# The router's pick with its scores, keys and sums in PSUM

## The chip, the cores and the metric

The kernel runs on one core of one Trainium2 chip. The metric is device time in microseconds (us) for one execution of the whole program, the median over several runs. One further execution was taken with the hardware profiler; every duration of a single instruction below is from that execution.

The engines are named as in the profile: PE is TensorE (PEld its weight loads), DVE is VectorE, ACT is ScalarE, POOL is GpSimd, SP is SyncE, which only issues DMA transfers here.

## The reference

One layer of two parts, on 8 batches of 256 rows of 512 numbers (2,048 rows, called tokens below). All is float32.

```python
x = x + xattn(layernorm(x), k, fside, ctx, ctx, 8)
x = x + ffn(layernorm(x), gate_w, ...)

# xattn: a causal convolution of products, then a sum over one index
kv = vr[:, :, :, None, :] * x2r[:, :, None, :, :]
y = irfft(rfft(kv) * k_f)[..., :L] + kv * skip
out = einsum('bhijl,bhil->bhjl', y, x1r)

# ffn: a shared expert, and the best two of eight experts for each token
scores = sigmoid(xf @ gate_w.T)
topk_w, topk_idx = top_k(scores, 2)
topk_w = topk_w / (topk_w.sum(-1, keepdims=True) + 1e-20) * 2.5
shared_out = silu(xf @ shared_wg.T) * (xf @ shared_wu.T) @ shared_wd.T
h = silu(einsum('td,efd->etf', xf, exp_wg)) * einsum('td,efd->etf', xf, exp_wu)
picked = einsum('etf,edf->etd', h, exp_wd)[topk_idx, arange(T)[:, None]]
routed_out = (topk_w[..., None] * picked).sum(axis=1)
```

## The kernel before

**Two stages.** In the first, up to about 462 us, a loop runs over the 32 heads of the convolution (`for h in range(H)`, L735). For each head, TensorE multiplies a Toeplitz tile by the products `kv` in ten matmuls that fill four PSUM tiles, `cv_0` to `cv_3` (`conv_products`, L306); GpSimd makes `kv` two heads ahead with four multiplications (`make_kv`, L292), and every other head the skip products with two more (L342, L344); VectorE weighs each PSUM tile with one multiplication and one reduction (`weigh`, L321: L326, L332). `ps_cv` has three buffers (L92), so a `cv` tile can be written once L326 has read the one three tiles before it. Between the heads TensorE does the matmuls of the shared expert (`up_step`, `down_step`). In the second stage the routed tokens are worked off in 39 blocks of 128 rows, each with the weights of its expert.

**The order is written out by hand** (`tc.manual_schedule()`, L79): each engine runs its instructions in the order of the program. What an instruction waits for is put in by the framework from the tiles that it reads and writes.

**The router** works on four chunks of 512 tokens (`NCHUNK`, L24). A chunk takes these steps, for chunks 0 to 2 inside the heads 10 to 14, 18 to 22 and 26 to 30, for chunk 3 after the last head:

- `route_logits` (L387) and `route_T` (L400): four small matmuls, a copy, and four transposes leave the logits' partial sums in a PSUM tile `plT`, tokens along the partitions.
- `route_pick` (L410), on VectorE but for one Sigmoid on ScalarE. On tiles of 128 partitions by 4 groups by 8 experts it finds the largest score (L429), marks where it stands (L430), multiplies by a falling `rank` so that the first of equals wins (L431, L432, L433), takes it out (L435) and does the same again; then the sum of both scores and its inverse (L437 to L440), the table's entries (L444, L445), the mask of picked experts (L448) and sums of the mask over the groups (L452).
- `route_ranks` (L457): two matmuls count in PSUM how many tokens before a token go to the same expert.
- `route_places` (L477): VectorE makes each token's place in the table, and GpSimd scatters the entries with eight indirect DMAs.

After chunk 3 the table is loaded again (`load_table`, L652), and `slots` (L668) makes from it the rows that the blocks of the second stage gather.

**Where the pick stands in a head.** For head 12, 20 and 28, `route_pick` comes between the second and the third weighing:

```python
        weigh(h, 1, pss[1])
        ...
            if r == 2:
                route_pick(c)
        ...
        weigh(h, 2, pss[2])
        ...
        weigh(h, 3, pss[3])
```

`ps_tp` (L94) is a ring of two PSUM buffers, used in turn by the transposes of the residual (`ptr`, L375), `pl`, `plT`, the ranks (`rk`, L460), every other product of the shared expert's second half, and `slots_ps`. The pick's own tiles (`score`, `left`, `key`, `best`, `top`, `sel`, `den`, `entry`, `mask`, `before`) are all in SBUF, in a pool of two buffers.

Of the kernel before, what the change touches and what calls it, by code (L numbers as in the profile page):

```python
# [11 lines left out]
ALU = mybir.AluOpType  # L12
AX = mybir.AxisListType
PE = mybir.EngineType.PE

P = 128
# [6 lines left out]
NLB = L // P  # L23
NCHUNK = 4  # L24
TPC = NT // NCHUNK
TC = TPC * P
NEXP = 8
# [17 lines left out]
SCALE = 2.5  # L45
# [3 lines left out]
def tile_xattn_moe(  # L49
# [28 lines left out]
    V, G, A, T, S = nc.vector, nc.gpsimd, nc.scalar, nc.tensor, nc.sync  # L78
# [97 lines left out]
    place = const.tile([P, NEXP], F32, name="place")  # L176
# [207 lines left out]
    lg, plT, picks = {}, {}, {}  # L384
# [20 lines left out]
    shape = [P, TPC, NEXP]  # L405

    def along(t):
        return t.unsqueeze(2).to_broadcast(shape)

    def route_pick(c):  # L410
        def rt(name, s=shape, dtype=F32):
            return small.tile(s, dtype, tag=name, name=f"{name}_{c}")

        logit = rt("logit")
        V.tensor_reduce(
            logit,
            plT.pop(c).rearrange("p i (k e) -> p i e k", k=NLB)[:, :, :NEXP, :],
            AX.X,
            ALU.add,
        )  # L420
        score = rt("score")
        A.activation(score, logit, AF.Sigmoid)
        left, key, best = rt("left"), rt("key"), rt("best", [P, TPC])
        top, sel = [], []
        for n in range(2):
            src = left if n else score
            top.append(rt(f"top{n}", [P, TPC]))
            sel.append(rt(f"sel{n}"))
            V.tensor_reduce(top[n], src, AX.X, ALU.max)  # L429
            V.tensor_tensor(key, src, along(top[n]), ALU.is_equal)  # L430
            V.tensor_tensor(key, key, rank.unsqueeze(1).to_broadcast(shape), ALU.mult)  # L431
            V.tensor_reduce(best, key, AX.X, ALU.max)  # L432
            V.tensor_tensor(sel[n], key, along(best), ALU.is_equal)  # L433
            if n == 0:
                V.scalar_tensor_tensor(left, sel[0], -2.0, score, ALU.mult, ALU.add)  # L435
        den = rt("den", [P, TPC])
        V.tensor_tensor(den, top[0], top[1], ALU.add)  # L437
        V.tensor_scalar_add(den, den, 1e-20)
        V.reciprocal(den, den)
        V.tensor_scalar_mul(den, den, SCALE)  # L440

        entry = rt("entry", [P, TPC, 2, 2])
        for n in range(2):
            V.tensor_copy(entry[:, :, n, 0], tokoff[:, c * TPC : (c + 1) * TPC])  # L444
            V.tensor_tensor(entry[:, :, n, 1], top[n], den, ALU.mult)  # L445
        mask = rt("mask", [P, TPC + 1, NEXP])
        V.memset(mask[:, TPC], 0.0)
        V.tensor_tensor(mask[:, :TPC], sel[0], sel[1], ALU.add)  # L448
        before = rt("before", [P, TPC + 1, NEXP])
        V.memset(before[:, 0], 0.0)  # L450
        for i in range(TPC):
            V.tensor_tensor(before[:, i + 1], before[:, i], mask[:, i], ALU.add)  # L452
        picks[c] = (sel, entry, mask, before)
# [23 lines left out]
    def route_places(c):  # L477
        def rt(name, s=shape, dtype=F32):
            return small.tile(s, dtype, tag=name, name=f"{name}_{c}")

        sel, entry, _, _ = picks.pop(c)
        ps = ranks.pop(c)
        pos = rt("pos")
        V.tensor_tensor(
            pos, ps[:, :TPC], place.unsqueeze(1).to_broadcast(shape), ALU.add
        )
        V.tensor_tensor(place, place, ps[:, TPC], ALU.add)
        for n in range(2):
            at, to = rt("at"), rt(f"to{n}", [P, TPC], I32)
            V.tensor_tensor(at, pos, sel[n], ALU.mult)  # L490
            with nc.allow_low_precision(reason="whole numbers below 2**14"):
                V.tensor_reduce(to, at, AX.X, ALU.add)
            for i in range(TPC):
                ins = G.indirect_dma_start(  # L494
                    out=table,
                    out_offset=bass.IndirectOffsetOnAxis(ap=to[:, i : i + 1], axis=0),
                    in_=entry[:, i, n, :],
                    in_offset=None,
                    bounds_check=P * NCOL - 1,
                    oob_is_err=True,  # L500
                )
                tc.declare_no_dep(ins.ins, group="table", reason="no two rows have one place")
                tc.add_to_no_dep_group("table", ins.ins)
                scatters.append(ins)
# [230 lines left out]
    for h in range(H):  # L735
# [39 lines left out]
        c, r = divmod(h - 10, 8)  # L775
        if c >= 0:
            if r == 2:
                route_pick(c)
            if r == 4:
                route_places(c)  # L780
# [49 lines left out]
    step()  # L830
    route_T(last_c)
    route_pick(last_c)
    settle()
    step()
    route_ranks(last_c)
    route_places(last_c)
    ek, pick, used = block_experts()
    tab = load_table()
# [246 lines left out]
```

## Time and profile before

| what | value |
|---|---|
| median of 3 runs | 825.37 us (824.21 to 828.68) |
| the profiled execution | 827.25 us in all, of it 825.5 us from the first to the last instruction (the span) |
| mean granted clock of TensorE | 0.99 |
| TensorE matmuls L312 (the convolution) | 640 records, 283.5 us |
| VectorE L326 and L332 | 128 each, 87.3 and 87.8 us |
| GpSimd L298 (`kv`) | 128, 132.4 us, 1067 ns each |

The first part of the profile's page gives each engine's busy time, its share of the span and its instructions. In the list of waits a row reads: engine, tile and line that waited, after the arrow whom it waited for, then the total in us, how often, and the longest. In a timeline a row reads: start in us from the span's start, duration in us, engine, line, operation, the tile written, an arrow, the tiles read, the shapes, how many instructions are merged into the row, and in brackets the engine's idle time just before and what ended it. A VectorE duration runs from the start of the instruction to its end and includes time in which it is held up after it has started.

### The profile page before, as it was taken

What the parts mean: (1) busy time and instruction counts of PE and PEld (TensorE: products, weight loads), DVE (VectorE), ACT (ScalarE), POOL (GpSimd) and SP (SyncE); (2) the same over time, 40 slices, a digit from 0 to 9 for tenths busy, and PEclk for the clock granted to TensorE, in tenths of its full rate; (3) what the DMA queues carried; (4) which work ended last, traced back from release to release, by engine and by line L of the source; (5) the groups of instructions that cost most, each with busy time, mean ns of one, the idle gap of its engine ahead of it and who ended that gap; (6) DMA issues with size and microseconds to landing.
All of it is one profiled execution on the core that took longest, in us unless ns stands there. A gap on an engine that the chain in (4) does not pass through costs nothing. (4 is left out here: it accounts for less than half of the span.)

```text
span 825.5 us, 7804 instructions
## 1 busy us (share of the span) xinstructions
PE 796.1 (96%) x2143; PEld 388.2 (47%) x2143; DVE 565.2 (68%) x1356; ACT 117.1 (14%) x180; POOL 429.3 (52%) x425
## 2 busy tenths in 40 slices
PE   8989999999999999999999999999999999999991
PEld 4434444444444444444444444455555555555550
DVE  4869966958745958755784625349888888888860
ACT  2000111111102120012120020001111111111110
POOL 7956652319532506815412103575777777777621
PEclk9999999999999999999999999999999999999996
DMA  6473333022432030330210187159333444333332
GB/s 217 160 260 114 118 112 103 25 89 49 135 110 90 26 103 13 134 109 25 65 38 1 51 332 267 36 180 252 72 71 73 77 74 74 74 71 69 65 41 35
DMA packets 52139, 82.77 MB, mean 100 GB/s; under 512 B 8832, under 2 KB 24064, under 8 KB 50944
## 3 DMA queue, kind: packets, MB, share of 16 engines
q1 hardware_dynamic: 36960, 55.48, 20.6%
q0 software_dynamic: 10816, 18.92, 12.3%
q10 hardware_dynamic: 4320, 7.87, 2.6%
q8 instruction: 19, 0.31, 0.1%
q14 instruction: 24, 0.20, 0.1%
HBM read 60.05 MB, written 22.18 MB: 100 GB/s over the span
## 5 line engine op out<-in xcount | busy, mean ns | idle before, releaser
L312 PE MATMUL cv<-kv,tz 128*128 128x512 f32 x640 | 283.5, 598 | 10.0 <-DVE prod L326 8.1
L312 PEld LDWEIGHTS cv<-kv,tz 128*128 128x128 f32 x640 | 119.6, 191 | 158.9 <-issue 125.2
L298 POOL TENSOR_TENSOR kv<-vT,ctxT 128x512 f32<-128x512 f32 x128 | 132.4, 1067 | 92.8 <-PE cv L312 76.9
L855 POOL DMA_INDIRECT xg<-xn_d,src x144 | 146.8, 1019 | 56.6 <-issue 38.5
L914 PE MATMUL up<-wgu_sb,xT 128*128 (+1 forms) x576 | 176.1, 459 | 0.0
L522 PE MATMUL gu<-xfT,wsh 128*128 128x512 f32 x352 | 154.4, 593 | 0.0
L958 DVE STREAM_TRANSPOSE hTb<-h 32x96 f32<-32x96 f32 (+1 forms) x560 | 146.3, 261 | 8.2
L914 PEld LDWEIGHTS up<-wgu_sb,xT 128*128 128x128 f32 x576 | 109.1, 190 | 70.6 <-issue 16.4
L494 POOL DMA_INDIRECT table<-entry,to x32 | 31.8, 995 | 143.0 <-DVE at L490 134.5
L522 PEld LDWEIGHTS gu<-xfT,wsh 128*128 128x128 f32 x352 | 66.6, 190 | 83.1 <-issue 82.6
L326 DVE TENSOR_TENSOR prod<-cv,ctxT 128x512 f32<-128x512 f32 x128 | 87.3, 682 | 23.7 <-PE cv L312 22.4
L972 PE MATMUL y<-wd_sb,hTb 128*128 (+3 forms) x216 | 98.6, 593 | 0.8 <-ACT hTb L947 0.8
L332 DVE TENSOR_REDUCE convT<-prod 128x64 f32<-128x512 f32 x128 | 87.8, 686 | 4.4
L981 POOL DMA_INDIRECT out_dram<-ys,row x36 | 58.2, 1616 | 42.8 <-issue 20.1
L567 PE MATMUL dn<-wshd,hT 128*128 128x512 f32 x160 | 70.6, 593 | 0.0
L972 PEld LDWEIGHTS y<-wd_sb,hTb 128*128 128x128 f32 (+1 forms) x216 | 41.0, 190 | 43.1 <-issue 34.9
L567 PEld LDWEIGHTS dn<-wshd,hT 128*128 128x128 f32 x160 | 30.2, 190 | 37.6 <-issue 37.6
L923 DVE TENSOR_TENSOR h<-h,up 128x352 f32<-128x352 f32 x36 | 18.6, 517 | 41.3 <-ACT h L922 41.3
L539 DVE TENSOR_TENSOR sg<-sg,gu 128x512 f32<-128x512 f32 (+1 forms) x24 | 16.4, 684 | 41.8 <-ACT sg L536 41.8
L361 POOL TENSOR_TENSOR skip<-ctxT,w 128x512 f32<-128x512 f32 x16 | 17.7, 1108 | 47.7 <-DVE w L356 47.7
L922 ACT ACTIVATE h<-up 128x352 f32<-128x352 f32 x36 | 16.7, 463 | 164.4 <-PE up L914 164.4
L536 ACT ACTIVATE sg<-gu 128x512 f32<-128x512 f32 (+1 forms) x24 | 14.3, 596 | 178.6 <-PE gu L522 178.5
(131 smaller groups left out, 421.9 us busy)
## 6 DMA issues: line engine op xcount, KB each, us to landing
wgu_sb<-in_egu_dram SPq DMA_DIRECT2D x8, 1408.0 KB, 16.7
x<-in_x_dram SPq DMA_DIRECT2D x32, 256.0 KB, 3.8
tz<-in_toep_dram SPq DMA_DIRECT2D x32, 256.0 KB, 2.7
ctxT<-in_cT_dram SPq DMA_DIRECT2D x16, 256.0 KB, 4.0
xn_d<-xn ACTq DMA_DIRECT2D x16, 256.0 KB, 2.0
out_dram<-x SPq DMA_DIRECT2D x16, 256.0 KB, 2.2
wd_sb<-in_ed_dram SPq DMA_DIRECT2D x8, 512.0 KB, 12.0
xq_f<-xn_d SPq DMA_DIRECT2D x60, 64.0 KB, 2.0
```

The source lines that it names most:

```text
L298: G.tensor_tensor(kv[:, mb], vT[t][:, mb, :, cols].unsqueeze(2).to_broadcast([P, B, NH, NH]), ctxT[t][:, mb, :, cols].unsqueeze(3).to_broa ...
L312: T.matmul(ps.rearrange("p b j i -> p (b j i)"), lhsT=tz[:, (lb - mb) * P : (lb - mb + 1) * P], rhs=kv[:, mb].rearrange("p b j i -> p (b j ...
L326: V.tensor_tensor(prod, ps, ctxT[t][:, lb, :, cols].unsqueeze(2).to_broadcast([P, B, NH, NH]), ALU.mult,)
L332: V.tensor_reduce(convT[t][:, lb, :, cols], prod, AX.X, ALU.add)
L494: ins = G.indirect_dma_start(out=table, out_offset=bass.IndirectOffsetOnAxis(ap=to[:, i : i + 1], axis=0), in_=entry[:, i, n, :], in_offse ...
L522: T.matmul(ps, lhsT=wsh[:, k, m0 : m0 + m], rhs=rhs[k], start=(k == 0), stop=(k == NLB - 1))
L567: T.matmul(ps, lhsT=hTs[c][:, ft, i * P : (i + 1) * P], rhs=wshd[:, ft, :], start=(ft == 0), stop=False,)
L855: G.indirect_dma_start(out=xgs[k][:, c, :], out_offset=None, in_=xn_q, in_offset=bass.IndirectOffsetOnAxis(ap=src[:, c, k : k + 1], axis=0 ...
L914: T.matmul(ps[:, m, :FF], lhsT=xTs[k][:, j].rearrange("p c b -> p (c b)"), rhs=wk[:, bass.ds(eks[k] * NGU + (m * NLB + j) * FF, FF)], star ...
L958: V.transpose(hT[q * Q : (q + 1) * Q, :n, c], hk[c * Q : (c + 1) * Q, q * NF * Q : (q * NF + n) * Q].rearrange("p (t a) -> p t a", a=Q),)
L972: T.matmul(ps, lhsT=hT[:fw, ft].rearrange("p c b -> p (c b)"), rhs=wk[:fw, bass.ds(eks[k] * NWD + ft * L, L)], start=(ft == 0), stop=(ft = ...
L981: G.indirect_dma_start(out=out, out_offset=bass.IndirectOffsetOnAxis(ap=row[:, k : k + 1], axis=0), in_=y, in_offset=None, bounds_check=NT ...
```

## The change

It is confined to `route_pick` and `route_places`. The score, what is left of it, and the keys are views of the chunk's own PSUM tile `plT`, at columns 0, 32 and 64 of each group's 128; the second top's sum and the denominator lie at columns 96 and 97. The second top is taken twice: once into SBUF, for the entries, once into PSUM, for the sum. The addition of 1e-20 and the scaling are one instruction with the constant 1/SCALE ahead of the inverse. The comparison that gives `sel[1]` is done a second time in place on `key`, so that the mask has an operand in PSUM. In `route_places`, `pos` is written over the ranks in PSUM. VectorE issues 28 instructions in a pick where it issued 27. The order of the instructions of all other engines stays; the Sigmoid's output is now in PSUM.

```diff
+        ps = plT.pop(c)
+
+        def pt(n, m=NEXP):
+            return ps[:, :, 32 * n : 32 * n + m]
+
         logit = rt("logit")
         V.tensor_reduce(
             logit,
-            plT.pop(c).rearrange("p i (k e) -> p i e k", k=NLB)[:, :, :NEXP, :],
+            ps.rearrange("p i (k e) -> p i e k", k=NLB)[:, :, :NEXP, :],
             AX.X,
             ALU.add,
         )
-        score = rt("score")
+        score, left, key = pt(0), pt(1), pt(2)
         A.activation(score, logit, AF.Sigmoid)
-        left, key, best = rt("left"), rt("key"), rt("best", [P, TPC])
+        best = rt("best", [P, TPC])
...
-        den = rt("den", [P, TPC])
-        V.tensor_tensor(den, top[0], top[1], ALU.add)
-        V.tensor_scalar_add(den, den, 1e-20)
+        second, den = pt(3, 1)[:, :, 0], ps[:, :, 3 * 32 + 1]
+        V.tensor_reduce(second, left, AX.X, ALU.max)
+        V.tensor_tensor(den, top[0], second, ALU.add)
+        V.tensor_scalar(den, den, 1e-20, 1.0 / SCALE, ALU.add, ALU.mult)
         V.reciprocal(den, den)
-        V.tensor_scalar_mul(den, den, SCALE)
...
-        V.tensor_tensor(mask[:, :TPC], sel[0], sel[1], ALU.add)
+        V.tensor_tensor(key, key, along(best), ALU.is_equal)
+        V.tensor_tensor(mask[:, :TPC], sel[0], key, ALU.add)
...
-        pos = rt("pos")
-        V.tensor_tensor(
-            pos, ps[:, :TPC], place.unsqueeze(1).to_broadcast(shape), ALU.add
-        )
+        pos = ps[:, :TPC]
+        V.tensor_tensor(pos, pos, place.unsqueeze(1).to_broadcast(shape), ALU.add)
```

## The prediction

> **What bounds it now.** I read the page's first part, then TensorE's list of waits, then the timelines of TensorE, VectorE and GpSimd around one pick.
>
> ```profile
> PE 796.1 (96%) x2143; PEld 388.2 (47%) x2143; DVE 565.2 (68%) x1356; ACT 117.1 (14%) x180; POOL 429.3 (52%) x425
> PE cv L312 <- DVE prod L326: 8.1, 4, 3.7
> 154.39 7.99 PE L312 MATMUL cv<-kv,tz 128*128 128x512 f32 x18 [1.40 <-DVE prod L326]
> 286.50 7.99 PE L312 MATMUL cv<-kv,tz 128*128 128x512 f32 x18 [1.40 <-DVE prod L326]
> 418.60 7.99 PE L312 MATMUL cv<-kv,tz 128*128 128x512 f32 x18 [1.63 <-DVE prod L326]
> ```
>
> TensorE is the bound: it is busy 96% of the span, at a granted clock of 0.99. VectorE's own time is worth something only where TensorE waits for it. That is 8.1 us in four waits: one at 58 us, long before the first pick, and the three shown. Each of the three stands just behind a pick (142, 274 and 406 us): head h's products are weighed in the order 0, 1, pick, 2, 3 (L781 follows L778), and the next head's second product needs the PSUM buffer that L326 frees for product 2. With three buffers, TensorE is one head's first product ahead and stops. The fourth chunk's pick (492 us) has no such wait.
>
> Why the picks of chunks 0 to 2 are long is in two timelines, VectorE's and, last two rows, GpSimd's:
>
> ```profile
> 142.16 0.19 DVE L429 TENSOR_REDUCE top<-score 128x4 f32<-128x32 f32 x1 [0.30 <-ACT score L422]
> 142.38 0.98 DVE L430 TENSOR_TENSOR key<-score,top 128x32 f32<-128x32 f32 x1
> 143.40 0.99 DVE L431 TENSOR_TENSOR key<-key,rank 128x32 f32<-128x32 f32 x1
> 144.42 0.19 DVE L432 TENSOR_REDUCE best<-key 128x4 f32<-128x32 f32 x1
> 144.64 0.77 DVE L433 TENSOR_TENSOR sel<-key,best 128x32 f32<-128x32 f32 x1
> ...
> 152.97 0.77 DVE L452 TENSOR_TENSOR before<-before,mask 128x8 f32<-128x8 f32 x4
> 153.65 0.68 DVE L326 TENSOR_TENSOR prod<-cv,ctxT 128x512 f32<-128x512 f32 x1
> 142.25 1.06 POOL L298 TENSOR_TENSOR kv<-vT,ctxT 128x512 f32<-128x512 f32 x1
> 150.96 1.07 POOL L298 TENSOR_TENSOR kv<-vT,ctxT 128x512 f32<-128x512 f32 x1
> ```
>
> GpSimd works without a pause from 141.23 to 152.03 (ten instructions). A VectorE step with two SBUF operands starting inside one of them ends about 0.05 us after it: L430 ends 143.36, GpSimd's instruction 143.31. Nine steps wait so in each pick (L430, L431 and L433 twice, L435, L437, L438). In chunk 3, with GpSimd idle, the same steps take 0.16 to 0.19 us and start 0.22 us apart.
>
> **The change, part by part.**
>
> *The wait that goes.* Scores, remaining scores, keys and sums lie in PSUM, so L430 to L438 have one SBUF operand at most. Does such a step escape? L326 multiplies a PSUM tile by an SBUF one; at 42.12 it ran beside GpSimd's kv (42.13 to 43.20) in 0.68 us, its usual time. So yes.
>
> *Price of a step on PSUM.* No row of before writes PSUM from VectorE or ScalarE. Reading it: L484 takes 154 ns for 128x32 out of PSUM, against 182 ns for L490, SBUF alone; at 512 elements L326 has 682 and L369, undisturbed, 680. [...] I take chunk 3's 0.22 us pitch[...].
>
> *What is added.* One VectorE instruction per chunk: `second` and the repeated comparison are added, the scaling is merged into L438. Some 0.22 us. ScalarE writes the scores to PSUM; I keep its 229 ns.
>
> *What moves into GpSimd's stretch.* Not all steps lose their second operand. The four sums `before` (L452) still read two SBUF tiles, and the two copies of `tokoff` (L444) go from SBUF to SBUF. In before they ran after 152.03, free. [...] the trace shows no copy beside GpSimd, so the nearest row is the one-source L213: at 40.93, 64.06 and 99.40 it got in at the next border between two kv instructions, but at 194.63 and 326.73, after GpSimd's indirect DMAs, it took 4.91 and 4.67 us. No indirect DMA directly precedes the picks, so I take one border.
>
> *The sum for chunk 0.* Fourteen steps from 142.16 to the reciprocal bring the first copy to 145.31, at the border of kv (ends 145.36) and skip (L342, 145.32 to 146.58). If it misses, it ends 146.63; the second copy meets L344 (146.66 to 147.92) and ends 147.97. Key and mask (no wait) to 148.5; the four sums end behind the four kv borders, 148.99, 150.02, 151.0 and 152.05. L326 then starts at 151.97. If the first copy gets in at 145.36, everything is one instruction earlier and L326 starts at 150.97. Before: 153.65. So VectorE gains 1.7 or 2.7 us, not the seven that nine waits of some 0.8 us suggest: six waits come back.
>
> *What TensorE gets.* Its last two matmuls before the stop start at 151.97; at its pitch of 0.43 us the next could start at 152.83 and did at 154.39. That is 1.56 us lost; likewise 1.57 (286.50 less 284.93) and 1.79 (418.60 less 416.81): 4.92 us. L326 with its 0.68 and 0.06 us to the release must start by 152.09, and both cases do. Next in line is product 3's buffer: freed two steps later, at 154.0 at most, needed after four matmuls at 154.55. kv, Toeplitz tiles and norms are paced by TensorE and move with it. So the whole 4.9 us goes.
>
> *Chunk 3*[...]. Before: sums end near 496.8, L539 and L541 follow to 498.13, and `pos` (L484) waits for TensorE's rank product until 498.83. Cover: 0.7 us less the added 0.22. By the row nothing shows. [...] `pos` in PSUM: L490 meets an idle GpSimd, nothing.
>
> *Buffers.* The pick's PSUM tile is held until the mask instead of L415. Next in its slot is the rank product, which needs the mask anyway. No wait.
>
> Span 825.5 less 4.9 is **820.6**. That execution took 827.25 in all, 1.7 outside the span and 0.2% over the median of the runs, 825.37; I take 4.9 off the median: **820.5 us**.
>
> **Rivals.**
> - *The copies starve.* If a copy cannot enter between two kv instructions, as L213 could not at 194.63, the first waits for L342's end, the second until GpSimd is idle at 152.03; copy to L326 takes 1.07 us in before, plus 0.2 for the extra step: L326 at some 153.2, TensorE at 153.95. Gain 0.45 a chunk, 1.4 in all: 824.0. For it: the 4.9 us row. Against: three of five passed, and those three had kv instructions of 1.06 us as around the picks, the two others 1.08 to 1.10.
> - *Smaller gain.* Part of the stall stays (the 152.09 limit is passed by only 0.12 us)[...]: about 822.5.
> - *Slower: the PSUM round trip.* If writing PSUM and reading it back makes each of the nineteen steps 0.25 us dearer (0.44 for 0.19), the slip is 4.7 us. In chunks 0 to 2 the sums would then start after GpSimd has finished; L326 comes at 153.9, a loss of about 0.2 each. In chunk 3 the slip less the cover, 4.3 us, goes straight to the table. Total 830. It decides from about 3.7 us of slip, 0.2 us a step. Against: no VectorE step on PSUM of this size takes over 0.29 us, the first reduce of 128 elements included.
> - *Nothing changes*, because PSUM steps wait for GpSimd too: 825.6. The L326 row speaks against it.
>
> **How the numbers follow.** Full gain 70%, smaller gain 13%, starved copies 10%, no effect 3%, slower 4%. What this kernel's measurement can tell from no change is 0.5%, 4.1 us: a time under 821.2 counts as faster. The full gain of 4.9 passes that narrowly; with runs that scatter by a microsecond it falls short about one time in six. Faster 0.60, same 0.35, slower 0.05. Range: from 818.8 (forecast, runs a little low) to 824.0 (starved copies).
>
> **What would show it.** TensorE's wait for L326 falls from 8.1 us in four waits to 3.7 in one. L430 to L438 take 0.15 to 0.22 us in every chunk; L444's copies, or the sums of L452, take near 1 us in chunks 0 to 2; the first L326 behind the pick starts 1.7 or 2.7 us earlier after the pick's first reduce. A copy of 4 to 5 us shows the first rival, steps of 0.4 us the slower one. I am wrong if TensorE's wait behind the picks stays, or goes and another of the same length stands after it.

## The result and the profile after

| | before | after |
|---|---|---|
| median of 12 runs each | 826.41 us (824.21 to 828.68) | 821.41 us (819.63 to 824.99) |
| ratio after to before, 95% interval | | 0.9946 (0.993 to 0.9963) |
| span of the profiled execution | 825.5 us | 821.7 us |
| VectorE busy in it | 565.2 us | 558.0 us |
| first pick: from its first reduction to the next L326 | 11.49 us | 8.76 us |

The kernel is 5.0 us faster; 820.5 us had been forecast. Below: from the page of the changed kernel, the engines' busy times; from TensorE's list of waits, the first row and the one for the table.

```profile
PE 796.9 (97%) x2143; PEld 388.9 (47%) x2143; DVE 558.0 (68%) x1360; ACT 117.0 (14%) x180; POOL 429.2 (52%) x425
PE cv L312 <- DVE prod L326: 2.6, 1, 2.6
...
PE slots_ps L689 <- DMA tab<-table: 1.2, 1, 1.2
```

TensorE's four waits for L326 have become one, the one at 57 us that has nothing to do with a pick. The three behind the picks are gone. Lines from L415 on have moved: L430 to L433 of before are L437 to L440 now, L444 is L451, L452 is L460.

The pick of chunk 0 in the timelines of the changed kernel, VectorE first, then GpSimd, then TensorE:

```profile
141.20 0.19 DVE L436 TENSOR_REDUCE top<-plT 128x4 f32<-128x32 f32 x1 [0.33 <-ACT plT L429]
141.43 0.20 DVE L437 TENSOR_TENSOR plT<-plT,top 128x32 f32<-128x32 f32 x1
141.66 0.20 DVE L438 TENSOR_TENSOR plT<-plT,rank 128x32 f32<-128x32 f32 x1
...
144.45 1.17 DVE L451 COPY entry<-tokoff 128x4 f32<-128x4 f32 x1
145.54 0.15 DVE L452 TENSOR_TENSOR entry<-top,plT 128x4 f32<-128x4 f32 x1
145.60 0.16 DVE L451 COPY entry<-tokoff 128x4 f32<-128x4 f32 x1
...
146.33 3.70 DVE L460 TENSOR_TENSOR before<-before,mask 128x8 f32<-128x8 f32 x4
149.96 0.68 DVE L326 TENSOR_TENSOR prod<-cv,ctxT 128x512 f32<-128x512 f32 x1
144.33 1.26 POOL L342 TENSOR_TENSOR skip<-vT,ctxT 128x512 f32<-128x512 f32 x1
145.67 1.27 POOL L344 TENSOR_TENSOR skip<-skip,skip_sb 128x512 f32<-128x512 f32 x1
150.98 4.46 PE L312 MATMUL cv<-kv,tz 128*128 128x512 f32 x10
```

The steps with an operand in PSUM take 0.20 us beside a busy GpSimd, where they took almost 1 us. Not all waits are gone: the first copy ends where GpSimd's L342 ends (145.59), and the four sums take 0.93 us each instead of 0.19. The second copy starts in the 0.08 us between L342 and L344, the second of which needs the first's result, and does not wait. L326 starts at 149.96, and TensorE runs from 150.98 without a stop.

**Where 3.8 us of span come from.** GpSimd's kv beside each pick waits for TensorE (11.00 us for `cv` at the first one, before and after) and so marks its progress. Before and after, it starts at 141.23 and 140.24, at 273.33 and 270.69, at 405.20 and 400.90; the last chunk's rank product runs at 498.26 and 492.06. The lead grows from 0.99 (the wait at 57 us was 1.1 us shorter in this execution) to 6.20: the picks gave 1.65, 1.66 and 1.90, **5.2 us**, against the 4.9 of the forecast. Of this lead 2.4 us are lost again in this one execution: the wait for the table was 1.19 us and not 0.46, and TensorE's clock then fell. Stretches of the changed kernel; the columns are the stretch and its length, busy us of TensorE, weight loads, VectorE, ScalarE and GpSimd with their counts, then the granted clock:

```profile
515.00:516.00 1.00, 1.00 (x10) 1.00 (x10) 0.00 (x0) 0.00 (x0) 0.00 (x0) 0.98 0.00 0
516.00:517.00 1.00, 1.00 (x2) 0.49 (x2) 0.90 (x5) 0.00 (x0) 0.00 (x0) 0.50 0.00 0
...
519.00:521.00 2.00, 2.00 (x5) 0.82 (x4) 0.00 (x0) 0.00 (x0) 1.68 (x2) 0.91 0.22 70
```

From just before 516 to 519.4, some 3.4 us, the clock is at half and costs 1.7 us; before ran the same work at 1.00. So 6.2 less 0.7 less 1.7 is 3.8. The longer wait for the table does not come from the pick: the last of chunk 3's scatters, which fill the table, starts 10.80 us behind TensorE's rank product, and did so 10.82 us behind it before. In a second profiled execution of the changed kernel the table came after 0.91 us without such a fall (the eight L528 records behind it take 3.68 us there and 5.38 here), and the span was 819.1.

### The profile page after: what moved, and what is told of

It reads as the page before. It is cut to its first block, busy times and chain, and to the rows that moved or that the text cites. A ratio compares the mean times of both kernels' runs of the same rounds, so it can differ in the third digit from the quotient of the medians.

```text
span 821.7 us, 7811 instructions
## 1 busy us (share of the span) xinstructions
PE 796.9 (97%) x2143; PEld 388.9 (47%) x2143; DVE 558.0 (68%) x1360; ACT 117.0 (14%) x180; POOL 429.2 (52%) x425
## 5 line engine op out<-in xcount | busy, mean ns | idle before, releaser
L861 POOL DMA_INDIRECT xg<-xn_d,src x144 | 146.8, 1019 | 57.1 <-issue 37.8
L528 PE MATMUL gu<-xfT,wsh 128*128 128x512 f32 x352 | 156.1, 598 | 0.0
L528 PEld LDWEIGHTS gu<-xfT,wsh 128*128 128x128 f32 x352 | 67.2, 192 | 84.2 <-issue 83.7
L326 DVE TENSOR_TENSOR prod<-cv,ctxT 128x512 f32<-128x512 f32 x128 | 87.3, 682 | 23.5 <-PE cv L312 22.1
L545 DVE TENSOR_TENSOR sg<-sg,gu 128x512 f32<-128x512 f32 (+1 forms) x24 | 16.4, 684 | 46.0 <-ACT sg L542 46.0
L598 DVE TENSOR_TENSOR x<-dn,x 128x512 f32<-128x512 f32 x16 | 10.3, 686 | 45.6 <-PE dn L586 45.6
L542 ACT ACTIVATE sg<-gu 128x512 f32<-128x512 f32 (+1 forms) x24 | 14.3, 596 | 183.8 <-PE gu L528 183.8
```

The source lines that it names most:

```text
L326: V.tensor_tensor(prod, ps, ctxT[t][:, lb, :, cols].unsqueeze(2).to_broadcast([P, B, NH, NH]), ALU.mult,)
L528: T.matmul(ps, lhsT=wsh[:, k, m0 : m0 + m], rhs=rhs[k], start=(k == 0), stop=(k == NLB - 1))
L861: G.indirect_dma_start(out=xgs[k][:, c, :], out_offset=None, in_=xn_q, in_offset=bass.IndirectOffsetOnAxis(ap=src[:, c, k : k + 1], axis=0 ...
```

## The experiments

Theory A, the prediction's: only the three stops of TensorE count; they come from L326 standing in VectorE's queue behind a slow pick, and are gone as soon as L326 starts within about 9.9 us of the pick's first reduction. Theory B: VectorE's own time counts, and the gain follows the waits removed.

**The changed kernel again**, unedited, as a reference.

> The changed kernel once more, as the reference for the other runs on this chip. Ratio to before near 0.9945 (about 4.5 to 5 us less). TensorE's waits behind the three picks are gone; the wait at 57 us (2.6 us there) and the wait for the table (1.2 us there) are the two that I expect to vary between executions by about 1 us, since neither touches the change.

Ratio 0.9932 (0.9909 to 0.9956); median 821.16 us. L326 at 8.76 us in all three picks again, no wait behind a pick, 2.3 us at 56 us, 0.9 us for the table.

**The order alone.** The kernel before, all of its pick in SBUF:

```diff
-            if r == 2:
-                route_pick(c)
...
         weigh(h, 3, pss[3])
+        if c >= 0 and r == 2:
+            route_pick(c)
```

> The kernel BEFORE, all of the pick in SBUF, with only its place changed: route_pick stands behind the head's fourth weighing instead of between the second and the third. Theory A (the gain is the three stalls of TensorE and nothing else; they come from L326 standing behind a slow pick): products 2 and 3 are weighed before the pick, their buffers come free in time, the three stalls go, and the time is that of the changed kernel, ratio to before 0.994 to 0.9955, although VectorE's steps wait for GpSimd as before. Each pick is a little cheaper, since it starts later and GpSimd still ends at 152. The next limit is tight: product 0 of the next head must be read by about 157.1 and is read by about 156.9. Theory B (VectorE's own time counts, what matters is that the steps stop waiting): no or little gain, ratio 0.998 to 1.000.

Ratio 0.9931 (0.9908 to 0.9954), median 820.77 us: the whole gain, without PSUM. VectorE's and TensorE's timelines:

```profile
144.34 1.00 DVE L430 TENSOR_TENSOR key<-score,top 128x32 f32<-128x32 f32 x1
145.37 0.99 DVE L431 TENSOR_TENSOR key<-key,rank 128x32 f32<-128x32 f32 x1
149.32 8.75 PE L312 MATMUL cv<-kv,tz 128*128 128x512 f32 x20
```

The first steps still wait a full GpSimd instruction each; but products 2 and 3 have been weighed before, and TensorE does all ten matmuls (twenty records) of the next head without a stop. This is what A expected. It does not yet rule out B: the moved pick runs on into the time when GpSimd is idle (from 149.4), so it is 7.86 us long instead of 11.49, and VectorE saves time here too. The next run separates the two.

**No waits left in the pick.**

```diff
-            V.tensor_copy(entry[:, :, n, 0], tokoff[:, c * TPC : (c + 1) * TPC])
+            A.copy(entry[:, :, n, 0], tokoff[:, c * TPC : (c + 1) * TPC])
...
-        V.tensor_tensor(mask[:, :TPC], sel[0], key, ALU.add)
+        V.tensor_tensor(key, sel[0], key, ALU.add)
+        V.tensor_copy(mask[:, :TPC], key)
...
-            V.tensor_tensor(before[:, i + 1], before[:, i], mask[:, i], ALU.add)
+            V.tensor_tensor(before[:, i + 1], before[:, i], key[:, i], ALU.add)
```

> The changed kernel with the five waits that are left in each pick taken away too: the token numbers are copied into the entries by ScalarE, the mask is built in PSUM and copied to SBUF, and the running sums read the mask from PSUM. Theory A: VectorE is done with the pick some 3.5 to 4 us earlier in chunks 0 to 2 (L326 about 5.3 us behind the pick's first reduction instead of 8.8) and TensorE gains nothing, since it no longer waits there: ratio to before as the changed kernel within 0.1%. Theory B: another third to half of the gain comes on top, ratio about 0.991 to 0.992.

L326 stands 5.02 us behind the first reduction, VectorE is busy 548.0 us, ten less than in the changed kernel, and the ratio is 0.9947 (0.9932 to 0.9962), median 823.39 us: no gain. B, which asked for 0.991 to 0.992, is out. But the run is not "as the changed kernel within 0.1%" either: the median is 2.2 us above that of the reference on the same chip, and though the intervals of the two ratios overlap, eight of its 13 runs are longer than the longest of the reference's six. Its profile shows a part of this. Around the heads 15 and 23 three small waits are new (0.30, 0.17 and 0.18 us), the latter two behind L213, which takes 4.91 us in the changed kernel's head 15; and the wait for the table is 1.35 us, 0.16 longer than in the changed kernel. Together that is 0.8 us. The eight L529 records behind the table take 5.37 us in this profile, as in the changed kernel's at half clock (5.38), and not 3.68 as in before; whether that belongs to the edit stays open. TensorE's list of waits, its timeline, and VectorE's:

```profile
PE cv L312 <- DVE prod L326: 2.9, 4, 2.4
200.80 1.55 PE L312 MATMUL cv<-kv,tz 128*128 128x512 f32 x3 [0.17 <-DVE prod L326]
191.96 5.54 DVE L213 TENSOR_SCALAR rstd<-mv 128x2 f32<-128x2 f32 x1
```

**Sum and denominator back in SBUF.**

```diff
-        second, den = pt(3, 1)[:, :, 0], ps[:, :, 3 * 32 + 1]
-        V.tensor_reduce(second, left, AX.X, ALU.max)
-        V.tensor_tensor(den, top[0], second, ALU.add)
+        den = rt("den", [P, TPC])
+        V.tensor_tensor(den, top[0], top[1], ALU.add)
```

> The changed kernel with the sum of the two tops and the denominator back in SBUF (the merged scaling stays); the second reduction that the PSUM sum needed is gone. Two waits for GpSimd come back in each pick. Theory A, by the grid of GpSimd's instructions: the first L326 behind the pick starts about 10 us after the pick's first reduction (8.76 in the changed kernel, 11.49 in before); the limit for TensorE is about 9.9; so the stalls are 0 to 0.2 us each and the time is that of the changed kernel within 0.7 us. Theory B: two of nine waits back, about a quarter of the gain lost, ratio about 0.9957.

L326 at 9.98, 9.96 and 9.98 us, no stop behind a pick, ratio 0.9939 (0.9919 to 0.9959). Two waits are back (in chunk 0 the sum takes 0.79 us and L445 1.20, where both took 0.17) and cost nothing. (Both theories' ratios lie in the interval; the trace decides.)

**Keys back in SBUF.**

```diff
-        score, left, key = pt(0), pt(1), pt(2)
+        score, left, key = pt(0), pt(1), rt("key")
```

> The changed kernel with only the keys back in SBUF; scores, what is left of them, and the sums stay in PSUM. Six steps of each pick read two SBUF tiles again (both multiplications by rank, both selections, the repeated comparison, the mask). Theory A, by the grid of GpSimd's instructions: the first L326 behind the pick starts about 10.3 us after the pick's first reduction, 0.45 us past the limit of 9.9, so three stalls of about 0.3 to 0.5 us come back: about 1.4 us more than the changed kernel, ratio to before 0.9955 to 0.9965. Theory B (gain in proportion to the waits removed): six waits back, two thirds of the gain lost, ratio about 0.998.

**Twelve idle steps** in chunks 0 to 2 of the changed kernel:

```diff
+        if c < NCHUNK - 1:
+            idle = rt("idle", [P, TPC])
+            for _ in range(12):
+                V.tensor_reduce(idle, key, AX.X, ALU.max)
         picks[c] = (sel, entry, mask, before)
```

> The changed kernel with twelve added reductions of a PSUM tile, which do nothing useful and wait for nobody, behind the running sums of chunks 0 to 2: about 2.7 us of VectorE time in each pick. Theory A: L326 comes about 11.4 us after the pick's first reduction, 1.5 us past the limit, and the stalls of 1.4 to 1.6 us are back though no step waits for GpSimd more than in the changed kernel: ratio to before 1.000 within 0.15%. A rival, that the stalls come from contention on SBUF itself (GpSimd's kv being late), expects the changed kernel's time, 0.9945.

TensorE's timeline behind the first pick, first with the keys in SBUF, then with the idle steps:

```profile
152.56 7.99 PE L312 MATMUL cv<-kv,tz 128*128 128x512 f32 x18 [0.31 <-DVE prod L326]
```

```profile
153.09 7.99 PE L312 MATMUL cv<-kv,tz 128*128 128x512 f32 x18 [1.25 <-DVE prod L326]
```

The kernels with the pick in its old place, side by side (the time is that from the pick's first reduction to L326, the stop is TensorE's idle time behind the pick, both for chunk 0):

| kernel | L326 after | stop | ratio to before |
|---|---|---|---|
| no waits left | 5.02 | none | 0.9947 (0.9932 to 0.9962) |
| the changed kernel | 8.76 | none | 0.9946 (0.993 to 0.9963) |
| sum and denominator in SBUF | 9.98 | none | 0.9939 (0.9919 to 0.9959) |
| keys in SBUF | 10.37 | 0.31 | 0.9945 (0.993 to 0.996) |
| twelve idle steps | 11.32 | 1.25 | 1.0004 (0.9992 to 1.0016) |
| before | 11.49 | 1.40 | 1 |

The stop grows by 0.97 us for each us of lateness ((1.40 less 0.31) over (11.49 less 10.37)) and begins at 10.05; the forecast had the limit at 9.93. With the keys in SBUF the stop was as expected, 0.31 us behind each pick; the ratio came out just under the 0.9955 to 0.9965 expected, in an interval that holds part of that, so three stops of this size show in the trace and not in the time. The idle steps bring the old time back though GpSimd is no more in the way than in the changed kernel: what TensorE waits for is L326's place in the queue, not SBUF.

**The last long stop.** The wait at 57 us has the same form: in head 4 the two transposes of L248 wait for DMAs, and L326 of products 2 and 3 stands behind them. (These DMAs read what ScalarE's queue stores, `xv_d` and `xn_d`; the store of `xv_d` issued at 43.2 us takes 7.4 us to land, where the median of all 14 is 2.0. The loads of the shared weights are under way then: issued from 36.3 to 37.8 us, ahead of the transposes' own DMAs in SyncE's queue (from 50.6), they take 9.3 and 14.3 to 14.5 us. That the one delays the other is not shown; no run tests it.) VectorE's and TensorE's timelines of the changed kernel:

```profile
54.11 0.71 DVE L248 STREAM_TRANSPOSE vT<-xq_v 128x512 f32<-128x512 f32 x1 [4.03 <-DMA xq_v<-xv_d]
56.05 0.71 DVE L248 STREAM_TRANSPOSE xfT<-xq_f 128x512 f32<-128x512 f32 x1 [1.23 <-DMA xq_f<-xn_d]
56.68 0.65 DVE L326 TENSOR_TENSOR prod<-cv,ctxT 128x512 f32<-128x512 f32 x1
57.39 4.97 PE L312 MATMUL cv<-kv,tz 128*128 128x512 f32 x7 [2.62 <-DVE prod L326]
```

The changed kernel with:

```diff
-        if not odd and t > 0:
+        if not odd and t > 0 and h != 4:
...
         weigh(h, 3, pss[3])
+        if h == 4:
+            square_vT(t + 1)
+            square_xfT(t - 2)
```

> The changed kernel with the last long wait of TensorE taken up in the same way: in head 4 alone the two transposes of L248, which wait for DMAs that stand behind the load of the shared expert's weights, come behind the head's four weighings instead of ahead of the third. Theory A: L326 of products 2 and 3 no longer stands behind them, TensorE's wait at 57 us (2.6 us in the changed kernel, 3.7 in before) goes, and the time is 2.6 to 3.7 us below the changed kernel, ratio to before about 0.990 to 0.9915. Rival: the wait only moves, since the next head's first product is weighed behind the same transposes, or kv of head 6 comes late from GpSimd: no gain beyond 0.9945.

Ratio 0.9901 (0.9881 to 0.9921), median 819.85 us: faster than the kernel before, and below the changed kernel's 0.9946 (0.993 to 0.9963), though the interval of that kernel's second measurement (0.9909 to 0.9956) overlaps. TensorE's timeline has head 5 in one piece:

```profile
53.76 8.75 PE L312 MATMUL cv<-kv,tz 128*128 128x512 f32 x20
...
64.38 6.04 PE L312 MATMUL cv<-kv,tz 128*128 128x512 f32 x13 [0.17 <-DVE prod L326]
```

**Both orders, no PSUM.** The kernel before with the two edits of order, and nothing else.

> The kernel BEFORE with two changes of order alone and nothing moved to PSUM: the pick behind the fourth weighing, and head 4's two transposes of L248 behind its weighings. Theory A: the same stalls are gone as with the changed kernel and the later transposes together, ratio to before 0.989 to 0.9915. If PSUM brings something that the order doesn't, this one stays 0.2% or more behind that kernel.

Ratio 0.9892 (0.9873 to 0.9911). It ran on a chip on which the kernels are slower (before: 841.12 us, this: 832.25), so only the ratio can be compared. In this profile TensorE stops some 7 us in all at matmuls of the experts (L917: 3.7 us for VectorE's `h`, 3.5 us for nothing that the profile shows), which the lists of before and of the changed kernel do not have, and its mean granted clock is 0.984, where theirs are 0.990 and 0.988. The long stops of the first stage are gone, as TensorE's list of waits has it:

```profile
PE cv L312 <- DVE prod L326: 0.2, 1, 0.2
```

It is not behind the kernel that has PSUM as well.

**Why a one-source step waits so long.** The first rival had the copies starve as L213 did at 194.63 and, in the changed kernel, does at 191.98 (4.91 us). They did not. The changed kernel, with chunk 0's eight scatters left out and eight GpSimd multiplications of 128x512 in their place:

```diff
+            if c == 0:
+                scr = small.tile([P, TPC, P], F32, tag="scr", name=f"scr_{n}", bufs=1)
+                for i in range(TPC):
+                    G.tensor_tensor(
+                        scr,
+                        at[:, :, :1].to_broadcast([P, TPC, P]),
+                        ones.unsqueeze(1).to_broadcast([P, TPC, P]),
+                        ALU.mult,
+                    )
+                continue
             for i in range(TPC):
```

> The changed kernel with the eight scatters of chunk 0 left out (its tokens get no routed experts, so the output is not the reference's) and eight GpSimd multiplications of 128x512 in their place, so that GpSimd's kv of that stretch still runs beside VectorE. The question is why the one-source step L213 waited 4.9 us through five GpSimd instructions in heads 15 and 23, while the copies of the pick get in at the next border. Theory S: a GpSimd instruction that follows an indirect DMA leaves no gap to the next one; then L213 in head 15 (near 192 us) waits for one border, 1.3 us at most, while in head 23 (near 322 us), behind chunk 1's scatters, it still takes 4 to 5 us. Rival: it is only the moment at which L213 starts; then both stay at 4 to 5 us. If L213 in head 15 does not fall beside GpSimd's kv, it tells nothing.

Its VectorE and GpSimd timelines, first an L213 of head 3, then for heads 15 and 23 a row of each:

```profile
40.34 0.26 DVE L213 TENSOR_SCALAR rstd<-mv 128x2 f32<-128x2 f32 x1
190.91 0.90 DVE L213 TENSOR_SCALAR rstd<-mv 128x2 f32<-128x2 f32 x1
188.67 4.14 POOL L298 TENSOR_TENSOR kv<-vT,ctxT 128x512 f32<-128x512 f32 x4
320.81 4.91 DVE L213 TENSOR_SCALAR rstd<-mv 128x2 f32<-128x2 f32 x1
320.34 4.12 POOL L298 TENSOR_TENSOR kv<-vT,ctxT 128x512 f32<-128x512 f32 x4
```

In heads 15 and 23 L213 meets the four kv instructions. Without scatters ahead of them the step gets in at the next border (0.90 us), with scatters it waits for all four and L342 (4.91 us). The step of head 15 starts inside the third kv and that of head 23 inside the first, so the moment alone could still be the reason; but the step of head 3, with no scatters ahead, takes 0.26 us here at 40.34, and in the changed kernel, where it starts at 41.01 inside the first too (the four kv run from 40.19 to 44.33), 0.27 us. So it is the indirect DMAs just ahead that make the difference, as far as one run of this kernel shows; how they do it stays open.

## Why the prediction was right

- **The bound and the three stops**: right. They went, and nothing else gained: with the pick moved the whole gain is there without PSUM, with no waits left nothing comes on top, and with L326 made late again by idle steps it is gone.
- **A step with one operand in PSUM escapes GpSimd**: right, 0.20 us for 0.98. One of the nine waiting steps was misread: L438, which took 1.00 us beside GpSimd and 0.17 in chunk 3, has a single source (`den`), not two SBUF operands.
- **The price of a PSUM step**: close to the 0.22 us a step that the forecast took. Steps of 128x32 that write PSUM take 195 to 199 ns against 191 in SBUF (chunk 3, both undisturbed), steps that only read it 186 to 192, and the first ten steps 2.29 us for 2.23. The some 30 ns less that L484 had suggested (154 ns against 182) do not show.
- **Waits that come back**: six were counted, five came. Of the two starts forecast for L326, 1.7 or 2.7 us earlier, it was the better, 2.73, but not by the way that was forecast for it: the first copy missed the border, as in the worse case, and the second slipped through the gap behind L342, which the forecast had not counted on. That was luck; the gain did not hang on it, since one wait more, for a kv instruction of 1.04 us, would by estimate put L326 near 9.8 us, and at 9.98 TensorE still does not stop.
- **The size**: 4.9 us forecast in the picks, 5.2 measured there. The median came out 0.9 us above the forecast because that of the kernel before did so too (826.41 us over all runs, where the forecast started from 825.37). At each stop TensorE had lost another 0.1 us beyond what the last matmuls' pitch shows (1.65, 1.66 and 1.90 us for 1.56, 1.57 and 1.79).
- **Chunk 3**: 0.22 us was counted for one more instruction; from the first reduction to L545 it became 5.09 us for 4.55, 0.54 more. Behind each of the two added steps (L444, L455) the next starts 0.23 to 0.24 us after it, and the sum starts 0.46 us behind the second selection, where it started 0.11 behind it. The cover of 0.7 us was enough: `pos` now waits 0.19 us for the rank product.
- **The rivals**: starved copies, no effect and a dear PSUM round trip are all ruled out by the rows above. One reason given against starved copies did not hold: kv instructions of 1.06 us were said to let a step in and those of 1.08 to 1.10 not, yet at 191.98 L213 waits through four of 1.05 to 1.07. The wait for the table lies between 0.16 and 1.52 us in the profiles of the kernels with all their scatters, of them 0.46, 0.65 and 1.29 in the three kernels without PSUM; no dependence on the change shows.

## What to carry to other kernels

Where one engine bounds the time, ask which single instruction releases it and what stands ahead of that in its engine's queue; making the work ahead cheaper and moving it behind gave the same here (0.9946 and 0.9931 of the time before), and moving is one line. The gain ends where the wait ends, here with 1.3 us to spare, and VectorE time saved beyond it bought nothing. When some steps are freed from a contention, look at what slides into the contended stretch behind them (here one copy, 1.17 us for 0.16, and four sums, 3.70 us for 0.77).

## What was not expected of the hardware

- After indirect DMAs a one-source VectorE step (L213) took 4.67 to 5.54 us, through five GpSimd instructions and once six, where it otherwise waited for one (0.90 us without the scatters).
- TensorE's clock fell to half for 3.4 us after stops of very different length: after 1.19 us for the table and a dozen short matmuls (the changed kernel, above), and after 2.33 to 3.70 us at 57 us in six profiles, where the 38 records behind the stop took 18.3 us. In two others, with stops of 2.42 and 2.49 us there, these took 17.3 and 17.4 us, so no fall of that length shows; nor does one behind 1.36 us for the table in the kernel with the idle steps (3.68 us for the eight records behind it, as in before). So the length of the stop does not decide it alone; what does stays open.
